# The last attention block weighs behind its three transposes instead of ahead of them

## The chip, the core and the metric

The kernel runs on one NeuronCore of a Trainium2 chip, as one program. The core has five engines that run side by side and meet only through semaphores: TensorE (PE, matrix products, with its weight loads shown apart as PEld), VectorE (DVE), ScalarE (ACT), GpSimd (POOL) and SyncE (SP, here only a DMA queue). Each engine takes its instructions in the order in which the program issued them. Matrix products land in PSUM, eight banks of 128 partitions by 512 floats; DVE and ACT read them out.

The metric is the device time of one execution in microseconds (us), the median of several. "Faster" means less of it.

## What is computed

A stack of four "macaron" layers L0 to L3 over 8 sequences of 512 tokens with 128 features, all in float32. The change touches the attention of layer L3 alone:

```python
def _L3_attn_ref(x, Wq, bq, Wk, bk, Wv, bv):
    q = x @ Wq.T + bq        # likewise k and v; 16 heads of 8 features
    ...
    scores = jnp.einsum('bhqw,bhkw->bhqk', q, k) / jnp.sqrt(jnp.asarray(W, x.dtype))
    scores = jax.nn.softmax(scores, axis=-1)
    scores = jax.nn.softmax(scores, axis=-1)
    h = jnp.einsum('bhqk,bhkw->bhqw', scores, v)
    ...
x = x + 0.5 * _L3_ffn_ref(_layernorm(x, axis=-1), ...)
x = x + _L3_attn_ref(_layernorm(x, axis=-1), ...)
x = x + 0.5 * _L3_ffn_ref(_layernorm(x, axis=-1), ...)
```

The softmax is taken twice, one on top of the other. The feed-forward part picks two of eight experts for each token; its up and down matrices have no activation between them, so the kernel multiplies them together beforehand and applies one 128x128 matrix for each expert.

## The kernel before

`l3_block` (L1414) is the last of four stages. Its attention is cut into 128 units, `units = (b, i, g)`: sequence b of 8, query tile i of 4 (128 queries), head group g of 4 (four heads). One pass of the loop `for n in range(last + 20)` is called unit n here. The order of instructions on PE, ACT, DVE and POOL is exactly the order in which this loop calls its helpers; nothing reorders them. A unit's data takes three passes:

- `score(n, h)`, L1450: four products for the four heads of a group, two for each half h, into a PSUM tile `s` (tag `s1`, two buffers of two banks). Each uses 32 of PE's 128 rows.
- `maximum(n, h)`, L1454, DVE: the row maxima of half h, over 1024 columns.
- `soften(n, h)`, L1461, ACT: the first exponential, two for each half, with row sums. It frees the `s` buffer of its half.
- `norm(n, h)`, L1467 and L1470: reciprocal and scaling on DVE, one of the four scalings on POOL from unit 14 on. Half 1 is done one pass later.
- `turn(n, j)`, L1476, PE: head j's probabilities are transposed, four 128x128 blocks into one PSUM bank `tp` (tag `tp`, three buffers used in turn). Heads 0 to 2 are turned in pass n + 1, head 3 in pass n + 2.
- `again(n)`, L1482, ACT: the second exponential, from `tp` to SBUF tile `p2` (eight buffers), in pass n + 2. It frees the `tp` bank.
- `weigh(n)`, L1492, PE: 16 products of the value weights (32 columns each) with the four `p2` tiles, in pass n + 2, summed into a single PSUM bank `o` that holds the four head groups of one query tile. After the fourth group (g == 3) `o` is copied to the SBUF tile `os` on ACT; `self.scalar` does not issue that copy at once but puts it on the list `self.late`, which `put_off()` issues at two places of the pass.
- `back(b, i)`, L1503 to L1508: in the pass after that copy, `os` is transposed into a `tp` bank, divided by the sums on DVE and added to x on POOL.

Between these the loop calls `works(n)` and `works(n + 0.5)`, which issue the steps of a hand-written timetable: the feed-forward steps of finished sequences (whitening, a transpose `turned`, routing, choosing, and the expert products `yp`, L384, whose readers are L386 on DVE, two or four instructions), and the whitening, transpose, projections and values of the next sequence. Each such step that uses PE takes one buffer from the same ring of three `tp` banks (`bank` with tag `tp`) and gives it back when DVE or ACT has read it. From unit 28 to unit 119 each pass issues an expert step with two readers; every fourth pass also issues `back`.

One pass issues, on PE and in this order: scores of n, turn 3 of n-2, the steps of `works(n)`, the weighing of n-2, the steps of `works(n + 0.5)`, turns 0 to 2 of n-1. On DVE: norm half 1 of n-1, both maxima of n, the readers of the steps, norm half 0 of n. On ACT: the four second exponentials of n-2, the first exponentials of half 0, what was put off, the first exponentials of half 1, what was put off.

The ring of `tp` banks is handed out in the order turn 3, steps, turn 0, turn 1, turn 2. With three banks, each request waits for the reader of the request three before it.

Of the kernel before, what the change touches and what calls it, by code (L numbers as in the profile page):

```python
# [8 lines left out]
F32 = mybir.dt.float32  # L9
I32 = mybir.dt.int32  # L10
AF = mybir.ActivationFunctionType
# [5 lines left out]
P = 128  # L17
# [127 lines left out]
class Net:  # L145
# [1268 lines left out]
    def l3_block(self, w2, w3, out):  # L1414
# [10 lines left out]
        nc, tc, l3 = self.nc, self.tc, self.l3  # L1425
        with ExitStack() as c:
            pool = c.enter_context(tc.tile_pool(name="an", bufs=1))
            wk = c.enter_context(tc.tile_pool(name="anw", bufs=2))
# [13 lines left out]
            scores, maxima, rcs, probs, turns, expos, outs, ats = {}, {}, {}, {}, {}, {}, {}, {}  # L1442

            def score(n, h):
                b, i, g = units[n]
                q, k = qs[b % 2], ks[b % 2]
                s = scores[n, h] = ps.tile([P, 2, 512], F32, tag="s1", name="s1", bufs=2)
                for jj in range(2):
                    cut = slice(32 * (2 * h + jj), 32 * (2 * h + jj) + 32)
                    nc.tensor.matmul(s[:, jj, :], lhsT=q[cut, g, i * P : (i + 1) * P], rhs=k[cut, g, :], start=True, stop=True)  # L1450

            def maximum(n, h):
                nm = maxima[n, h] = wk.tile([P, 2], F32, tag="nm", name="nm", bufs=4)
                nc.vector.tensor_reduce(nm, scores[n, h], AX.X, ALU.max, negate=True)  # L1454

            def soften(n, h):
                s, nm = scores.pop((n, h)), maxima.pop((n, h))
                sm = rcs[n, h] = wk.tile([P, 2], F32, tag="sm", name="sm", bufs=4)
                for jj in range(2):
                    e = wk.tile([P, 512], F32, tag="e", name="e", bufs=12)  # L1460
                    nc.scalar.activation(e, s[:, jj, :], AF.Exp, bias=nm[:, jj : jj + 1], accum_out=sm[:, jj : jj + 1])  # L1461
                    probs.setdefault(n, []).append(e)

            def norm(n, h):

                rc = wk.tile([P, 2], F32, tag="rs", name="rs", bufs=4)
                nc.vector.reciprocal(rc, rcs.pop((n, h)))  # L1467
                for jj in range(2):
                    e = probs[n][2 * h + jj]
                    (nc.gpsimd if h and jj and n >= 14 else nc.vector).tensor_scalar(e, e, rc[:, jj : jj + 1], None, ALU.mult)  # L1470

            def turn(n, j):

                tp = ps.tile([P, 512], F32, name="tp", **turned).rearrange("p (a b) -> p a b", b=P)
                for kt in range(4):
                    nc.tensor.transpose(tp[:, kt, :], probs[n][j][:, kt * P : (kt + 1) * P], self.ident)  # L1476
                turns.setdefault(n, []).append(tp)

            def again(n):

                p = wk.tile([P, 4, P], F32, tag="p2", name="p2", bufs=8)
                nc.scalar.activation(p, turns[n].pop(0), AF.Exp)  # L1482
                expos.setdefault(n, []).append(p)

            def weigh(n):
                b, i, g = units[n]
                if g == 0:
                    outs[b, i] = ps.tile([P, 512], F32, tag="o", name="o")
                o, p2 = outs[b, i], expos.pop(n)
                for kt in range(4):  # L1490
                    for j in range(4):
                        nc.tensor.matmul(  # L1492
                            o[32 * j : 32 * j + 32, g * P : (g + 1) * P], lhsT=vas[b % 2][:, kt, 4 * g + j, :], rhs=p2[j][:, kt, :],
                            start=(kt == 0), stop=(kt == 3))
                if g == 3:
                    outs[b, i] = wk.tile([P, 512], F32, tag="os", name="os")
                    self.scalar(outs[b, i], o, AF.Copy)

            def back(b, i):
                os = outs.pop((b, i))  # L1500
# [9 lines left out]
            units = [(b, i, g) for b in range(NB) for i in range(4) for g in range(4)]  # L1510
            last = len(units)
# [25 lines left out]
            for b in range(NB):  # L1537
                n = 16 * b
                if b:
                    m = max(n - 20, 1)  # L1540
                    self.plan(todo, (m, m + 1, m + 2, m + 3, m + 4, n - 9, n - 7.5, n - 5, n - 4.5), *whiten(b), lambda xn: self.turned(xn, bank, self.longer()),
                              lambda xt, b=b: l3.project(b, 0, xt, bank), lambda xt, b=b: l3.project(b, 1, xt, bank),
                              lambda xt, b=b: l3.values(b, xt, bank))
# [9 lines left out]
            def works(at):  # L1553
                for work in todo.pop(at, ()):
                    work()
# [4 lines left out]
            def put_off():  # L1560
                works, self.late = self.late, []
                for work in works:
                    work()

            self.late = []
            with tc.manual_schedule(engines={*FIXED, mybir.EngineType.Pool}):
                for work in clear:
                    work()
                for n in range(last + 20):
                    here, prev, two = 0 <= n < last, 0 <= n - 1 < last, 0 <= n - 2 < last  # L1570
                    if n == last:
                        spare[0] = dict(tag="s1", bufs=2)
                    if here:
                        score(n, 0)
                        score(n, 1)
                    if two:
                        for j in range(4):
                            again(n - 2)
                            if j == 0:
                                turn(n - 2, 3)  # L1580
                    if prev:
                        norm(n - 1, 1)
                    if here:
                        maximum(n, 0)
                        maximum(n, 1)
                    works(n)
                    if here:
                        soften(n, 0)
                    put_off()
                    if two:  # L1590
                        weigh(n - 2)
                    works(n + 0.5)
                    if prev:
                        for j in range(3):
                            turn(n - 1, j)
                    if here:
                        soften(n, 1)
                        norm(n, 0)
                    put_off()
                assert not todo  # L1600
# [442 lines left out]
```

## Time and profile before

| | us |
|---|---|
| median of 3 runs | 2611.81 (2608.92 to 2611.95) |
| the profiled execution, its own time | 2632.98 |
| its span, first to last instruction | 2631.2 |
| L3 attention units: start of the scores of unit 0, 28, 119, 127 | 1878.35, 2040.45, 2541.76, 2588.95 |
| busy between 2041 and 2484 us (443 us): PE, PEld, DVE, ACT, POOL | 436.7, 291.8, 400.6, 403.6, 223.7 |
| granted TensorE clock in that stretch | 1.00 |

The profile is of one execution. "PE" rows are matrix products, whose ends are modelled and overlap; "PEld" rows are the weight loads ahead of them, whose starts show best when PE went on to the next group. A row of the timeline gives start, length, engine, line, operation, output <- inputs, a count when several were merged, and in brackets the idle time before it with what ended it.

### The profile page before, as it was taken

To read this page: it belongs to the slowest core of one execution; us is meant where nothing else is said; L and a number is where in the kernel's file an instruction comes from. 1 tells how busy PE (TensorE), PEld (TensorE's weight loads), DVE (VectorE), ACT (ScalarE), POOL (GpSimd) and SP (SyncE) were. 2 spreads that over 40 slices of the span, in tenths; PEclk is the share of its full clock that TensorE was granted. 3 is DMA by queue.
4 is the path that set the end of the run, shared out by engine and by line. 5 is a ranking of instruction groups with operands and counts; after the bars stand their busy time and mean duration, and the time that the engine had idled before them with its cause. 6 is when DMAs were issued, how large, how long until landed. Compare 5 with 4: busy or idle time off the path is not lost.

```text
span 2631.2 us, 51301 instructions
## 1 busy us (share of the span) xinstructions
PE 2389.5 (91%) x18184; PEld 1427.7 (54%) x18184; DVE 2024.7 (77%) x5597; ACT 1756.3 (67%) x4393; POOL 1154.0 (44%) x2003
## 2 busy tenths in 40 slices
PE   6858756999999998999999999999899999999997
PEld 6537533344444444566565655556565666666664
DVE  5347348888888866878788787877688989898897
ACT  2135134466677666766757676676598999999984
POOL 5655643244454452163452635332234545454443
PEclk9878877799999999999999999999899999999999
DMA  8121340001010100000000000000000000000000
GB/s 270 51 81 30 93 124 1 18 18 27 19 26 19 34 2 4 1 1 1 1 1 1 1 1 1 1 1 9 9 18 9 10 22 22 10 14 22 22 2 13
DMA packets 72962, 66.51 MB, mean 25 GB/s; under 512 B 15675, under 2 KB 62787, under 8 KB 70563
## 3 DMA queue, kind: packets, MB, share of 16 engines
q1 hardware_dynamic: 68096, 54.88, 7.7%
q0 software_dynamic: 3584, 7.58, 1.0%
q8 instruction: 145, 2.38, 0.4%
q10 hardware_dynamic: 1026, 0.78, 0.1%
q14 instruction: 111, 0.90, 0.1%
HBM read 36.47 MB, written 26.80 MB: 24 GB/s over the span
## 4 chain that ended last, share of the span: by engine, by line
PE 62%; DVE 20%; ACT 9%; POOL 4%; issue 3%; DMA 1%; another core or an unknown queue 0%; SPq 0%; POOLq 0%; DVEq 0%; ACTq 0%
PE tp L1476 8%; PE s L1450 6%; PE s L1290 5%; PE o L1757 4%; PE o L1492 4%; PE o L1320 4%; PE s L1706 4%; PE yp L384 3%; ACT e L1713 3%; PE s L1310 3%; DVE nm L1291 3%; DVE nm L1454 3%; PE tp L1732 2%; PE pp L1674 2%; PE hp L684 2%
## 5 line engine op out<-in xcount | busy, mean ns | idle before, releaser
L1461 ACT ACTIVATE e<-s,nm 128x512 f32<-128x512 f32 x512 | 345.4, 689 | 26.0 <-DVE nm L1454 21.4
L1291 DVE TENSOR_REDUCE nm<-s 128x2 f32<-128x1024 f32 x256 | 301.4, 1218 | 75.9 <-PE s L1310 61.0
L1454 DVE TENSOR_REDUCE nm<-s 128x2 f32<-128x1024 f32 x256 | 301.0, 1217 | 29.6 <-PE s L1450 27.7
L1482 ACT ACTIVATE p<-tp 128x512 f32<-128x512 f32 x512 | 279.3, 618 | 61.6 <-PE tp L1476 61.6
L1312 ACT ACTIVATE pr<-s 128x512 f32<-128x512 f32 x512 | 271.6, 600 | 73.1 <-PE s L1310 69.3
L1476 PE MATMUL tp<-cst,e 128*128 128x128 f32 x2048 | 294.3, 282 | 15.2 <-DVE rs L1467 7.9
L1476 PEld LDWEIGHTS tp<-cst,e 128*128 128x128 f32 x2048 | 221.5, 142 | 153.0 <-issue 86.8
L1470 POOL TENSOR_SCALAR e<-e,rs 128x512 f32<-128x512 f32 x114 | 200.1, 1755 | 229.8 <-DVE rs L1467 191.3
L1290 PE MATMUL s<-k,q 32*128 32x512 f32 x1024 | 279.2, 657 | 18.0 <-DVE nm L1291 14.6
L1310 PE MATMUL s<-q,k 32*128 32x512 f32 x1024 | 290.4, 627 | 5.4 <-DVE at L1333 4.4
L1713 ACT ACTIVATE e<-e,m 128x512 f32<-128x512 f32 (+3 forms) x512 | 286.1, 570 | 12.6 <-DVE m L1710 12.5
L1710 DVE CUSTOM_DVE_ANT_0 e<-s,bias 128x512 f32<-128x512 f32 (+3 forms) x512 | 220.1, 485 | 92.9 <-PE s L1706 92.4
L219 POOL TENSOR_TENSOR d<-st 128x4 f32<-128x4 f32 (+3 forms) x90 | 19.7, 218 | 554.2 <-DVE st L215 356.9
L1734 ACT COPY pt<-tp 128x512 f32<-128x512 f32 x320 | 174.5, 590 | 90.1 <-PE tp L1732 90.1
L386 DVE SCALAR_TENSOR_TENSOR x<-yp,sel,x 128x128 f32<-128x128 f32 x512 | 177.9, 348 | 39.7 <-PE yp L384 26.6
L1470 DVE TENSOR_SCALAR e<-e,rs 128x512 f32<-128x512 f32 x398 | 195.5, 521 | 9.1
L1743 DVE TENSOR_SCALAR e<-e,rc 128x512 f32<-128x512 f32 (+3 forms) x512 | 190.0, 416 | 9.1
L1732 PE MATMUL tp<-cst,e 128*128 128x128 f32 x1280 | 170.9, 278 | 9.8 <-ACT pt L1734 4.0
L1450 PE MATMUL s<-k,q 32*128 32x512 f32 x1024 | 174.8, 651 | 5.1 <-ACT e L1461 2.6
L1706 PE MATMUL s<-qk 64*128 64x512 f32 (+3 forms) x1024 | 173.6, 457 | 2.0 <-DVE m L1710 1.4
L1492 PE MATMUL o<-p,va 128*32 128x128 f32 x4096 | 165.8, 277 | 2.9 <-ACT p L1482 2.9
L1732 PEld LDWEIGHTS tp<-cst,e 128*128 128x128 f32 x1280 | 139.2, 141 | 48.5 <-issue 13.3
(467 smaller groups left out, 4848.0 us busy)
## 6 DMA issues: line engine op xcount, KB each, us to landing
yd<-z SPq DMA_DIRECT2D x8, 1024.0 KB
r<-yd SPq DMA_DIRECT2D x32, 256.0 KB
sk<-pu SPq DMA_DIRECT2D x16, 256.0 KB
k<-sk SPq DMA_DIRECT2D x60, 64.0 KB
w<-in_l_w SPq DMA_DIRECT2D x14, 256.0 KB
xd<-wqkv SPq DMA_DIRECT2D x12, 256.0 KB
x<-in_x SPq DMA_DIRECT2D x8, 256.0 KB
up<-in_l_up SPq DMA_DIRECT2D x8, 256.0 KB
```

Source lines behind the costliest of these rows:

```text
L1290: nc.tensor.matmul(s[:, jj, :], lhsT=q[cut, g, i * P : (i + 1) * P], rhs=k[cut, g, :], start=True, stop=True)
L1291: nc.vector.tensor_reduce(nms[b, g // 2][:, i, 2 * h : 2 * h + 2, g % 2], s, AX.X, ALU.max, negate=True)
L1310: nc.tensor.matmul(s, lhsT=k[cut, g, kt * P : (kt + 1) * P], rhs=q[cut, g, :], start=True, stop=True)
L1450: nc.tensor.matmul(s[:, jj, :], lhsT=q[cut, g, i * P : (i + 1) * P], rhs=k[cut, g, :], start=True, stop=True)
L1454: nc.vector.tensor_reduce(nm, scores[n, h], AX.X, ALU.max, negate=True)
L1461: nc.scalar.activation(e, s[:, jj, :], AF.Exp, bias=nm[:, jj : jj + 1], accum_out=sm[:, jj : jj + 1])
L1470: (nc.gpsimd if h and jj and n >= 14 else nc.vector).tensor_scalar(e, e, rc[:, jj : jj + 1], None, ALU.mult)
L1476: nc.tensor.transpose(tp[:, kt, :], probs[n][j][:, kt * P : (kt + 1) * P], self.ident)
L1482: nc.scalar.activation(p, turns[n].pop(0), AF.Exp)
L1706: nc.tensor.matmul(s[:, jj, 0:w], lhsT=qs[n][cut, i * P : (i + 1) * P], rhs=ks[n][cut, 0:w], start=True, stop=True)
L1713: outs.append(lambda e=e, jj=jj: nc.scalar.activation(e, e, AF.Exp, bias=mins[n][:, jj, i : i + 1], scale=-1.0, accum_out=sums[n][:, jj, i ...
L1732: nc.tensor.transpose(tp[:, k, :], block(n, jj, i, kt), self.ident)
```

## The change

The 16 products of `weigh(n - 2)` are issued behind `works(n + 0.5)` and turns 0 to 2, as the last thing of the pass on PE, so that the scores of n + 1 follow them. The copy of `o` to `os` is taken out of `weigh` into a function `leave`; it is issued in the next pass, on ACT, behind the first of the four second exponentials, and no longer put off. `back` stays in its pass, which is now the pass of the copy.

```diff
@@ weigh(n)
                             start=(kt == 0), stop=(kt == 3))
+
+            def leave(n):
+                b, i, g = units[n]
                 if g == 3:
-                    outs[b, i] = wk.tile([P, 512], F32, tag="os", name="os")
-                    self.scalar(outs[b, i], o, AF.Copy)
+                    o, outs[b, i] = outs[b, i], wk.tile([P, 512], F32, tag="os", name="os")
+                    nc.scalar.copy(outs[b, i], o)
@@ the loop over n
                             again(n - 2)
                             if j == 0:
                                 turn(n - 2, 3)
+                                if n > 2:
+                                    leave(n - 3)
+                    elif 3 <= n < last + 3:
+                        leave(n - 3)
...
                     put_off()
-                    if two:
-                        weigh(n - 2)
                     works(n + 0.5)
                     if prev:
                         for j in range(3):
                             turn(n - 1, j)
+                    if two:
+                        weigh(n - 2)
                     if here:
                         soften(n, 1)
                         norm(n, 0)
```

## Prediction

> **What bounds the kernel now.** I read the page first, for the shares, then the timeline of single units, weight loads and DVE side by side. The page says that PE is the busy engine and shows the groups of the L3 attention:
>
> ```profile
> PE 2389.5 (91%) x18184; PEld 1427.7 (54%) x18184; DVE 2024.7 (77%) x5597; ACT 1756.3 (67%) x4393; POOL 1154.0 (44%) x2003
> ...
> L1482 ACT ACTIVATE p<-tp 128x512 f32<-128x512 f32 x512 | 279.3, 618 | 61.6 <-PE tp L1476 61.6
> ...
> L1492 PE MATMUL o<-p,va 128*32 128x128 f32 x4096 | 165.8, 277 | 2.9 <-ACT p L1482 2.9
> ```
>
> A busy PE may be a waiting PE, so a single unit decides. Unit 44 (scores from 2129.19, next scores 2134.12), weight loads, then ACT:
>
> ```profile
> 2129.19 0.31 PEld L1450 LDWEIGHTS s<-k,q 32*128 32x128 f32 x8 [0.17 <-issue]
> 2130.26 0.42 PEld L1476 LDWEIGHTS tp<-cst,e 128*128 128x128 f32 x4 [0.76 <-issue]
> 2130.65 0.30 PEld L384 LDWEIGHTS yp<-wall,xt 128*128 128x128 f32 x2
> 2131.28 0.15 PEld L1492 LDWEIGHTS o<-p,va 128*32 128x32 f32 x6 [0.33 <-issue]
> 2131.67 0.79 PEld L1492 LDWEIGHTS o<-p,va 128*32 128x32 f32 x26 [0.23 <-ACT p L1482]
> 2132.66 1.29 PEld L1476 LDWEIGHTS tp<-cst,e 128*128 128x128 f32 x12 [0.20 <-issue]
> 2134.12 0.30 PEld L1450 LDWEIGHTS s<-k,q 32*128 32x128 f32 x4 [0.17 <-issue]
> ```
>
> ```profile
> 2131.02 0.60 ACT L1482 ACTIVATE p<-tp 128x512 f32<-128x512 f32 x1 [1.06 <-PE tp L1476]
> ```
>
> PE goes round from scores to scores with one wait: the weighing stops for the fourth second exponential, which needs turn 3, which follows the scores. This is what the change attacks. Now DVE in the same unit, and unit 16 (scores from 1968.97), whose expert step has four readers in place of two:
>
> ```profile
> 2130.37 2.35 DVE L1454 TENSOR_REDUCE nm<-s 128x2 f32<-128x1024 f32 x2 [0.23 <-PE s L1450]
> 2132.64 0.73 DVE L386 SCALAR_TENSOR_TENSOR x<-yp,sel,x 128x128 f32<-128x128 f32 x2
> ```
>
> ```profile
> 1972.44 1.50 DVE L386 SCALAR_TENSOR_TENSOR x<-yp,sel,x 128x128 f32<-128x128 f32 x4
> ```
>
> ```profile
> 1972.50 0.86 PEld L1476 LDWEIGHTS tp<-cst,e 128*128 128x128 f32 x8 [0.20 <-issue]
> 1974.06 0.42 PEld L1476 LDWEIGHTS tp<-cst,e 128*128 128x128 f32 x4 [0.70 <-PE tp L1476]
> 1974.64 0.31 PEld L1450 LDWEIGHTS s<-k,q 32*128 32x128 f32 x8 [0.17 <-issue]
> ```
>
> In unit 16 turns 0 and 1 run, but turn 2 stands still until 1974.06, 0.12 behind the end of L386 at 1973.94: the ring of three gives it the bank of the expert step, which DVE reads only behind both maxima. The label names PE, but the times fit DVE. In unit 44 that bank is free at 2133.37 and turn 2 begins at 2132.66 + 0.86 = 2133.52. The bank was late there too; the weighing stood in the time before it.
>
> **The change, step by step.** I count from a unit's scores S to the next S'.
>
> *Removed from the middle:* weighing, 32 weight loads in 0.81, and the wait for the fourth exponential (0.23 in unit 44). *Added at the end:* the same 0.81 between turn 2 and S'. Its neighbours change: turns to scores (0.17 in the rows) becomes turns to weighing (0.17 is the gap from other 128x128 loads to the weighing in units without an expert step) and weighing to scores. The trace has no weighing followed by scores. Bounds: 0 if the loads slip underneath, 0.20 by the gap from weighing to turns; I take 0.18, near the upper end, since each change of tile shape in these rows shows 0.17 to 0.20. So the tail behind turn 2 grows from 0.17 to 0.17 + 0.80 + 0.18 = 1.15, by 0.98.
>
> The Trainium skill, "TensorEngine Tiling (Array Packing)", Key Properties, says that a change of tiling mode drains the array. The 0.17 to 0.20 agree, and it would put a drain at weighing to scores and take one per unit away in the middle; for a PE that never waited for banks that would be a gain of about 0.2 a unit. By "no drain at the new place" the sum below would be some 20 us less. Against the change speaks "Perfetto Trace Analysis", Identifying Performance Opportunities: a gap that comes back again and again can mean too few PSUM buffers. Unit 16's 0.70 is such a gap, and the change gives the ring no bank, so by this rule the gap stays and the work that filled it is gone.
>
> *What the head start of turns 0 to 2 is worth:* nothing, when turn 2 waits. With one expert step of two readers: maxima from S + 1.18 (2130.37), L386 ends at S + 4.18 (2133.37), turn 2 at S + 4.30, its loads 0.42, then 1.15: S' = S + 5.87. Behind the waiting turn 2 on PE now stand the weighing and the next scores; for those wait maxima, turn 3, and through them every exponential. The next L386 stands behind those maxima, so this is a closed loop, and lateness is not made good in the next unit.
>
> - 48 units (28 to 118) issue just that step. They took 247.9 us, 5.16 each: 18 of them 4.92 as unit 44, the others to 5.4, being early at the scores and waiting for the first exponentials. After: 48 x 5.87 = 281.8, **+33.9**.
> - 18 units add `back`; its second reader ends at S + 4.67 (unit 50), so S' = 4.67 + 0.12 + 0.42 + 1.15 = 6.36. Before 97.4 (5.41 each), after 114.5, **+17.1**.
> - 25 units (five a sequence: transpose, projections, route, values) take two or three banks and already wait for the last. One set took 5.31 + 7.31 + 5.81 + 5.92 + 6.86 = 31.21. By the same rule with their own releases: 6.3 + 7.9 + 6.3 + 6.9 + 7.9 = 35.3. The two that gain part back: the second was 0.5 early at its scores, the third has its routing product sooner. 5 x 4.1, **+20.5**.
> - Units 6 to 27 (128.9 us): 20 of 22 have a step with a bank, at up to +1.0 each; the two without and four whose DVE readers are late for another reason gain part of it back. Estimate from the releases in each unit: **+14**. Units 119 to 126 (47.2 us) the same way: **+6**.
> - Ends: two of units 0 to 5 take a bank, and past unit 127 one weighing moves in front of turn 3 of the last unit: **+2.5**.
>
> *The copy.* 32 copies of 0.61 (L321 before) stay on ACT. They go from behind the first exponentials to behind the first second exponential. I cost the move at nothing: ACT waits there for turn 3 anyway (1.06 in the row above; 0.40 in units that are early). Without that cover it is 32 x 0.6 = 19 us. The weighing of the pass before must be done by then; it ends near S', and the copy is wanted by `back` at S' + 1.5. The single bank `o` is free well before the next weighing. No DMA moves, and POOL and SP queues keep their order; weighing is moved past half-step products and three turns on PE only.
>
> Sum: 33.9 + 17.1 + 20.5 + 14 + 6 + 2.5 = +94. On the profiled execution 2632.98 + 94 = 2727. The runs' median lies 21.2 below that execution, so 2611.8 + 94 = **2706 us** (+3.6%).
>
> **Rivals.**
>
> 1. *Milder loss.* The 48 units stay on their other loop (first exponential, scores, turn 3, fourth second exponential, first exponentials: about 5.3) because DVE reads the bank sooner. For: only 18 of them run at the bank's pace now. Against: DVE order is fixed and maxima follow the scores. Then only the rest pays: 94 - 33.9 = 60, 2672 us.
> 2. *No change.* Weighing was cover for nothing and is cover for nothing: PE has slack before the scores. For: the scores wait for ACT in the units of 5.3. Against: unit 16's 0.70. 2612 us.
> 3. *Faster.* The wait for the fourth exponential was the bound: place, first loads of L1492; price, 0.23 in a unit like 44 plus one change of tile shape less, 0.20: 0.43 x 126 = 54, so 2558 us. It decides if turn 2's bank is free by about S + 3.3, where turn 2 would then want it. For: the 61.6 us that ACT waits for turns. Against: the release at S + 4.18.
> 4. *Worse.* Every unit pays 0.98: 126 x 0.98 = 123, 2735 us.
>
> **How the numbers follow.** Forecast 0.82, milder 0.06, no change 0.04, faster 0.05, worse 0.03. The forecast's own spread: 73 without the gap at weighing to scores (about 115 units x 0.18 = 21 less), 113 if the copy loses its cover (+19). To hold 8 in 10 the range reaches down to the milder case: 2670 to 2725. What a measurement can tell from none is 0.2%, 5 us. Slower 0.91 (forecast, milder, worse), same 0.04, faster 0.05.
>
> **What would show it.** In the profile after, units 28 to 118 at 5.8 to 5.9 without and 6.3 to 6.4 with `back`; weight loads of turn 2 split off and begun 0.1 behind the end of L386; weighing in one group of 32 loads without a wait for ACT; scores no longer waiting for first exponentials; ACT and DVE idle longer, all for PE. The forecast is wrong if turn 2 runs with 0 and 1 in one group, or if the units stay near 5.2.

## The result, and the profile after

| | before, us | after, us |
|---|---|---|
| median | 2610.36 (2606.77 to 2611.95, 4 runs) | 2706.89 (2702.75 to 2711.83, 4 runs) |
| ratio | | 1.0374, 95% interval 1.0361 to 1.0386: slower |
| span of the profiled execution | 2631.2 | 2701.0 |
| scores of unit 0, of unit 127, by their first weight load | 1878.32, 2588.95 | 1850.70, 2657.61 |
| between them | 710.63 | 806.91 |
| from unit 127 to the end of the span | 42.3 | 43.4 |

The attention stage is longer by 96.3 us and the end by 1.1. The spans differ by less, 69.8, since the part ahead of the stage took 27.6 us less in the execution that was profiled after. The medians differ by 96.5. (The 1878.35 for unit 0 in the earlier table is its first product, not its first weight load.)

On the page of the changed kernel, the shares, the shares of the chain that ended last (engines, then lines), and groups; behind them the chain and two of the groups on the page before:

```profile
PE 2334.5 (86%) x18184; PEld 1398.5 (52%) x18184; DVE 2022.7 (75%) x5597; ACT 1766.2 (65%) x4393; POOL 1152.7 (43%) x2003
...
PE 55%; DVE 28%; ACT 9%; POOL 4%; issue 3%; DMA 1%; SPq 0%; ACTq 0%; DVEq 0%; POOLq 0%
DVE nm L1454 10%; PE s L1290 5%; PE s L1450 5%; PE o L1492 5%; PE tp L1476 4%; PE o L1764 4%; PE o L1320 4%; PE s L1713 3%; PE s L1310 3%; ACT e L1720 3%; DVE x L386 3%; DVE nm L1291 3%; PE tp L1739 2%; PE yp L384 2%; PE pp L1681 2%
...
L1476 PE MATMUL tp<-cst,e 128*128 128x128 f32 x2048 | 310.9, 283 | 156.1 <-DVE rs L1467 75.9
L1454 DVE TENSOR_REDUCE nm<-s 128x2 f32<-128x1024 f32 x256 | 301.4, 1219 | 134.0 <-PE s L1450 134.0
...
L1482 ACT ACTIVATE p<-tp 128x512 f32<-128x512 f32 x512 | 283.8, 612 | 133.1 <-PE tp L1476 130.0
```

```profile
PE 62%; DVE 20%; ACT 9%; POOL 4%; issue 3%; DMA 1%; another core or an unknown queue 0%; SPq 0%; POOLq 0%; DVEq 0%; ACTq 0%
...
L1454 DVE TENSOR_REDUCE nm<-s 128x2 f32<-128x1024 f32 x256 | 301.0, 1217 | 29.6 <-PE s L1450 27.7
...
L1476 PE MATMUL tp<-cst,e 128*128 128x128 f32 x2048 | 294.3, 282 | 15.2 <-DVE rs L1467 7.9
```

No engine got more work: the instruction counts are the same, no busy sum grew by more than 10 us, and PE's fell by 55. What grew is waiting. Turns waited 15.2 us before and 156.1 now; the maxima 29.6 and 134.0; the second exponentials 61.6 and 133.1. DVE's share of the chain rose from 20% to 28%, with the maxima (L1454) on top at 10%. The clock is not the cause: from unit 28 to unit 118, where 73.7 of the 96.3 us arise, it was 1.00 in both profiles. Engines wait for each other longer than before, and one unit shows for what.

Unit 44 after, weight loads, from its scores to the next:

```profile
2130.00 0.31 PEld L1450 LDWEIGHTS s<-k,q 32*128 32x128 f32 x8 [0.20 <-issue]
2131.07 0.42 PEld L1476 LDWEIGHTS tp<-cst,e 128*128 128x128 f32 x4 [0.76 <-issue]
2131.46 0.30 PEld L384 LDWEIGHTS yp<-wall,xt 128*128 128x128 f32 x2
2131.79 1.11 PEld L1476 LDWEIGHTS tp<-cst,e 128*128 128x128 f32 x8
2134.29 0.42 PEld L1476 LDWEIGHTS tp<-cst,e 128*128 128x128 f32 x4 [1.40 <-issue]
2134.88 0.81 PEld L1492 LDWEIGHTS o<-p,va 128*32 128x32 f32 x32 [0.17 <-issue]
2135.89 0.31 PEld L1450 LDWEIGHTS s<-k,q 32*128 32x128 f32 x8 [0.20 <-ACT p L1482]
```

The products of turn 2, DVE and ACT in the same unit:

```profile
2134.32 0.63 PE L1476 MATMUL tp<-cst,e 128*128 128x128 f32 x4 [1.19 <-DVE x L386]
```

```profile
2131.18 2.36 DVE L1454 TENSOR_REDUCE nm<-s 128x2 f32<-128x1024 f32 x2 [1.24 <-PE s L1450]
2133.45 0.73 DVE L386 SCALAR_TENSOR_TENSOR x<-yp,sel,x 128x128 f32<-128x128 f32 x2
```

```profile
2131.83 0.60 ACT L1482 ACTIVATE p<-tp 128x512 f32<-128x512 f32 x1 [2.07 <-PE tp L1476]
```

Turns 0 and 1 run early, as the change means them to, and then PE stands for 1.40. The label on the loads is "issue", but L386 ends at 2133.45 + 0.73 = 2134.18 and turn 2 begins 0.11 later; the row of its products names L386 on DVE. The weighing follows in one piece of 0.81, with no wait for ACT, and only behind it the next scores: 5.89 where the same unit took 4.93. The maxima had waited 1.24 for scores, the fourth second exponential 2.07 for turn 3. In every unit from 28 to 118 the weight loads of the scores run in one go (0.31, where before they took up to 0.81); the scores no longer wait for the first exponentials.

### The profile page after: what moved, and what is told of

Its sections match the earlier page's. It is cut to its first block, busy times and chain, and to the rows that moved or that the text cites. A ratio compares the mean times of both kernels' runs of the same rounds, so it can differ in the third digit from the quotient of the medians.

```text
span 2701.0 us, 51296 instructions
## 1 busy us (share of the span) xinstructions
PE 2334.5 (86%) x18184; PEld 1398.5 (52%) x18184; DVE 2022.7 (75%) x5597; ACT 1766.2 (65%) x4393; POOL 1152.7 (43%) x2003
## 4 chain that ended last, share of the span: by engine, by line
PE 55%; DVE 28%; ACT 9%; POOL 4%; issue 3%; DMA 1%; SPq 0%; ACTq 0%; DVEq 0%; POOLq 0%
DVE nm L1454 10%; PE s L1290 5%; PE s L1450 5%; PE o L1492 5%; PE tp L1476 4%; PE o L1764 4%; PE o L1320 4%; PE s L1713 3%; PE s L1310 3%; ACT e L1720 3%; DVE x L386 3%; DVE nm L1291 3%; PE tp L1739 2%; PE yp L384 2%; PE pp L1681 2%
## 5 line engine op out<-in xcount | busy, mean ns | idle before, releaser
L1476 PE MATMUL tp<-cst,e 128*128 128x128 f32 x2048 | 310.9, 283 | 156.1 <-DVE rs L1467 75.9
L1454 DVE TENSOR_REDUCE nm<-s 128x2 f32<-128x1024 f32 x256 | 301.4, 1219 | 134.0 <-PE s L1450 134.0
L1482 ACT ACTIVATE p<-tp 128x512 f32<-128x512 f32 x512 | 283.8, 612 | 133.1 <-PE tp L1476 130.0
L1290 PE MATMUL s<-k,q 32*128 32x512 f32 x1024 | 279.5, 659 | 18.0 <-DVE nm L1291 14.6
L386 DVE SCALAR_TENSOR_TENSOR x<-yp,sel,x 128x128 f32<-128x128 f32 x512 | 177.8, 348 | 39.0 <-PE yp L384 26.0
L1739 PE MATMUL tp<-cst,e 128*128 128x128 f32 x1280 | 170.9, 278 | 9.8 <-ACT pt L1741 4.0
L1739 PEld LDWEIGHTS tp<-cst,e 128*128 128x128 f32 x1280 | 139.2, 141 | 48.5 <-issue 13.1
L1290 PEld LDWEIGHTS s<-k,q 32*128 32x128 f32 x1024 | 88.6, 192 | 137.5 <-DVE nm L1291 100.1
L1450 PE MATMUL s<-k,q 32*128 32x512 f32 x1024 | 154.6, 653 | 5.3 <-ACT e L1461 2.6
```

Of the source, the lines that this page charges most:

```text
L1739: nc.tensor.transpose(tp[:, k, :], block(n, jj, i, kt), self.ident)
```

## The experiments

All times are medians, and ratios are to runs of the kernel before on the same chip: 2609.96 for the four kernels with one part alone or at another place, 2611.07 for the four with something left out, 2643.70 for the three run last. The unit times come from the weight loads of the scores in each profile.

### One part alone

`copy_alone`: the weighing back at its old place, only the copy moved.

```diff
                     put_off()
+                    if two:
+                        weigh(n - 2)
                     works(n + 0.5)
                     if prev:
                         for j in range(3):
                             turn(n - 1, j)
-                    if two:
-                        weigh(n - 2)
```

> Weighing stays at its old place, ahead of the half-step works and the three turns; only the copy of the weighed sums moves into the next pass, behind the first second exponential. Theory (the bare weighing behind turn 2 is the whole loss, the copy stands where ACT waits for turn 3): 2605 to 2617 us, as before. Rival (the copy's new place delays the second exponentials): 32 x 0.6 = 19 us more, 2630.

Measured 2609.17, ratio 0.9997 (0.9987 to 1.0006). The copy's move costs nothing by itself.

`weigh_alone`: the weighing behind the three turns, the copy put off as before.

> Only the weighing moves, behind the three turns; the copy is put off within the same pass as before, so ACT must wait for the weighing's end (about 0.2 us behind the next scores' start) before the second exponentials of the next pass: some 0.45 us later there, 32 times. Theory (the loop goes through maxima, readers, turn 2, weighing, scores and ACT has 0.7 us to spare in it): 2700 to 2715 us, as the changed kernel. Rival (the copy in its new place hides part of the loss, or causes it): 14 us more, 2721, or well under 2700.

Measured 2718.05, ratio 1.0417 (1.0397 to 1.0436). The weighing alone brings the whole loss, and 11 us more than the changed kernel; the theory's bound of 2715 was missed. Unit by unit, the profiles of the two agree to 0.02 from unit 3 to unit 120, and differ by 2.2 in units 121 and 122. So the two were run again side by side, on another chip.

> The changed kernel once more, in one call with the next. 2703 to 2711 us. In the profiles the units 0 to 127 took 806.9 us here and 809.3 with only the weighing moved, all of the 2.4 in units 121 and 122; the medians of the two lay 11 us apart, from different calls. Theory (the copy's place is worth those 2.4): 2 to 5 us between the two. Rival (it is worth 11): 8 to 14 us.

> Only the weighing moves, once more. Theory: 2 to 5 us over the changed kernel of the same call. Rival: 8 to 14 us over it.

Measured 2741.12 and 2743.69 where the kernel before took 2643.70: ratios 1.0370 (1.0356 to 1.0384) and 1.0385 (1.0371 to 1.0399). The gap is 2.6 us, though the two intervals overlap; the 11 did not come back, and the four runs of `weigh_alone` behind it had spread over 14 us (2707.47 to 2721.86). Units 119 to 126 took 54.4 and 56.6, as in the first pair of profiles. Units 28 to 118 took 575.1 and 578.3 in this pair; those 3.1 us lie in four units in which the clock fell (last section), and are not the copy's. The weight loads of turn 2 in unit 121, changed kernel and then `weigh_alone`:

```profile
2621.71 0.47 PEld L1476 LDWEIGHTS tp<-cst,e 128*128 128x128 f32 x4 [1.11 <-ACT p L1482]
```

```profile
2625.56 0.71 PEld L1476 LDWEIGHTS tp<-cst,e 128*128 128x128 f32 x4 [2.64 <-issue]
```

From the scores of the unit (2615.89 and 2618.21) that is 5.82 and 7.35. In the changed kernel turn 2 waits for the first second exponential of the next pass; in the other it waits for the four readers of an expert step, which end at 2625.44. In the changed kernel the same four readers end only at 2623.12, behind the start of turn 2. The semaphores that turn 2 waits for say the same: ACT's alone in the one, those of DVE and PE in the other. So the pool of PSUM tiles handed turn 2 a different bank, by these waits turn 0's instead of the expert step's. The ring is thus not strict, though "The kernel before" and the prediction take it to be so. The two kernels differ only in where the copy stands, and of the units from 3 on only 121 and 122 show a difference.

### The same work at two other places

`between_0_1` and `between_1_2`: the changed kernel with the weighing between two of the turns (k is 1 or 2).

```diff
                     if prev:
-                        for j in range(3):
+                        for j in range(k):
                             turn(n - 1, j)
                     if two:
                         weigh(n - 2)
+                    if prev:
+                        for j in range(k, 3):
+                            turn(n - 1, j)
```

> The changed kernel, but the weighing stands between turn 0 and turn 1. Theory (the loss is that nothing fills the wait of turns 1 and 2 for the bank of an expert step): the weighing fills it again, units of 4.9 to 5.4 us, 2600 to 2615 us in all. Rival (a later weighing costs by itself, by what waits for it, or by its neighbours on PE): 0.4 us or more a unit, over 2650.

> The changed kernel, but the weighing stands between turn 1 and turn 2. Theory: in the 48 units with one expert step only turn 2 waits for its bank, and the weighing fills that wait, 5.2 us each as before; in the 43 units with two or three banks turn 1 waits too, to about 4.3 us behind the scores, and the weighing behind it is bare, about 1.0 us each. Sum 2611 + 43 + some 5 in the first 28 units: 2645 to 2670 us. Rival (a later weighing costs by itself): all units pay, 2700; rival (any place ahead of turn 2 is as good): 2611.

Measured 2607.57, ratio 0.9986 (0.9977 to 0.9995), and 2652.67, ratio 1.0156 (1.0139 to 1.0174). Weight loads of `between_0_1`, unit 44:

```profile
2106.62 0.31 PEld L1450 LDWEIGHTS s<-k,q 32*128 32x128 f32 x8 [0.17 <-issue]
...
2108.40 0.57 PEld L1476 LDWEIGHTS tp<-cst,e 128*128 128x128 f32 x4
2109.15 0.81 PEld L1492 LDWEIGHTS o<-p,va 128*32 128x32 f32 x32 [0.17 <-issue]
2110.16 0.42 PEld L1476 LDWEIGHTS tp<-cst,e 128*128 128x128 f32 x4 [0.20 <-issue]
2110.91 0.42 PEld L1476 LDWEIGHTS tp<-cst,e 128*128 128x128 f32 x4 [0.34 <-PE tp L1476]
2111.50 0.30 PEld L1450 LDWEIGHTS s<-k,q 32*128 32x128 f32 x4 [0.17 <-issue]
```

The weighing stands in the time in which turn 2 waits for its bank; of that wait 0.34 is left and the unit takes 4.88. It also waits for no exponential, since turn 0 runs meanwhile. In `between_1_2` a unit with `back` (unit 50, scores from 2153.73) shows the other case:

```profile
2153.73 0.30 PEld L1450 LDWEIGHTS s<-k,q 32*128 32x128 f32 x4 [0.17 <-ACT e L1461]
...
2156.68 0.42 PEld L1476 LDWEIGHTS tp<-cst,e 128*128 128x128 f32 x4
2158.02 0.42 PEld L1476 LDWEIGHTS tp<-cst,e 128*128 128x128 f32 x4 [0.92 <-PE tp L1476]
2158.61 0.81 PEld L1492 LDWEIGHTS o<-p,va 128*32 128x32 f32 x32 [0.17 <-issue]
2159.62 0.42 PEld L1476 LDWEIGHTS tp<-cst,e 128*128 128x128 f32 x4 [0.20 <-issue]
2160.20 0.31 PEld L1450 LDWEIGHTS s<-k,q 32*128 32x128 f32 x8 [0.17 <-issue]
```

Two banks are taken here, so turn 1 waits already (0.92, to 0.11 behind the end of L386 at 2157.91) and the weighing behind it is bare: the unit takes 6.48, where the kernel before took 5.37. The 48 units with one expert step took 5.08 each (5.17 before), the 18 with `back` 6.56 (5.41), the 25 others 7.06 (6.24; 4.7 us of their sum are falls of the clock, last section). It is not lateness that costs: the weighing costs where it stands behind a turn that waits for DVE, and nothing where it stands ahead of one.

Of the versions that leave nothing out, `between_0_1` and the next are the only ones whose interval lies below the kernel before, `between_0_1` by 0.14%.

`mixed`: `between_0_1`, but in each fourth pass (`n % 4 == 2`) the weighing is ahead of turn 0.

> The weighing stands between turn 0 and turn 1, but ahead of turn 0 in each fourth pass, the one with the transposes of the weighed sums, where two banks are taken and the profile of the version between turn 0 and turn 1 shows 0.2 us more a unit than before (18 units, 3.8 us). Theory (those 18 units lose by it): 3 us less than that version, 2601 to 2606 us. Rival (those units only start earlier against the exponentials, which bound them): no gain, 2606 to 2610 us.

Measured 2638.28 on a chip on which the kernel before took 2643.70: ratio 0.9980 (0.9968 to 0.9992). The intervals of the two versions overlap, so the medians do not tell them apart. In the profiles units 0 to 127 took 705.0 against 705.9, which is not the 3 that the theory named: the 18 units with `back` took 5.56 each, against 5.62 in `between_0_1` and 5.41 before, and their neighbours stayed as they were. Of the 3.8 us that these units had lost 1.1 came back. Neither theory nor rival foresaw that, and what holds the rest is not shown.

### Less of the suspected costs

`half_before`, `half_after`: the same edit in both kernels; only two of the four key blocks are weighed.

```diff
-                for kt in range(4):
+                for kt in range(2):
...
-                            start=(kt == 0), stop=(kt == 3))
+                            start=(kt == 0), stop=(kt == 1))
```

> The kernel before with half of each weighing left out (8 of 16 products, two of the four key blocks), 0.40 us of PE less in each of 128 units. Theory (in the middle of the pass the weighing is cover for the wait of turn 2 for its bank, and the loop over the exponentials is as long): gains of 0.0 to 0.1 us a unit, 2598 to 2611 us. Rival (PE's work bounds the kernel before): 128 x 0.4 = 51 us, 2560.

> The changed kernel with the same half of each weighing left out. Theory (behind turn 2 nothing covers the weighing): 0.40 us less in nearly each unit, 45 to 51 us, 2656 to 2662. Rival (the loss is the changes of shape around the weighing, or the copy): under 10 us less, about 2700.

Measured 2601.85, ratio 0.9967 (0.9957 to 0.9977), and 2657.25, ratio 1.0174 (1.0146 to 1.0201). The same 0.43 us of PE work a unit (loads of 0.38 against 0.81 in unit 44 after) is worth 9 us before and, by the ratios, (1.0374 - 1.0174) x 2611 = 52 us after; in the profiles units 0 to 127 lost 7.2 and 48.5. Before, the 48 units with one expert step gained a quarter of it (5.06 against 5.17); after, all of it (5.46 against 5.89). The weighing was mostly covered and is bare.

`one_reader_before`, `one_reader_after`: the second of two DVE readers is left out.

```diff
-            for e in range(m):
+            for e in range(1 if m == 2 else m):
                 nc.vector.scalar_tensor_tensor(x[:, i, :], yp[:, e, :], ...)
```

> The kernel before with the second of the two DVE readers left out in every expert step of two (96 units), so that x gets half of these experts' products; the bank is free 0.36 us sooner. Theory (before, the bank decides only where two or three banks are taken; elsewhere the weighing or the exponentials do): 18 units gain up to 0.3, 20 units up to 0.36, the rest nothing: 2596 to 2609 us. Rival (bank bound everywhere already): 90 x 0.36 = 32 us, 2579.

> The changed kernel with the same reader left out. Theory (scores, maxima, readers, turn 2, weighing, scores is the loop): 0.36 us less in the 48 and the 18 units and in most of the 25, some 32 us, 2672 to 2679 us; a unit with one expert step takes 5.53. Rival (the place of the weighing costs by itself, whenever the bank is free): no change, 2707.

Measured 2600.82, ratio 0.9963 (0.9949 to 0.9978), and 2671.92, ratio 1.0220 (1.0196 to 1.0244). After, 40 us by the ratios (37.0 in units 0 to 127 of the profiles) where 32 were expected. Unit 44 of `one_reader_after`, DVE and turn 2:

```profile
2134.53 0.34 DVE L386 SCALAR_TENSOR_TENSOR x<-yp,sel,x 128x128 f32<-128x128 f32 x1
```

```profile
2134.93 0.42 PEld L1476 LDWEIGHTS tp<-cst,e 128*128 128x128 f32 x4 [0.95 <-DVE x L386]
```

The 48 units took 5.45, where 5.53 was expected and the changed kernel took 5.89: the reading fell from 0.73 to 0.34, by 0.39, and turn 2 followed it by 0.06, not 0.11. So freeing the bank sooner shortens the changed kernel unit by unit, though neither the weighing nor anything around it was touched; the rival falls. Before, the same edit gave 10 us, nearly all in the units with two or more banks (the 48 took 5.15 against 5.17).

## Why the prediction was right, and where its terms were off

Forecast 2706, measured 2706.9. That the two agree within 1 us is partly luck: the terms are 3.4 us short in sum, and the four runs spread over 9 us. The terms, by the starts of the scores in the two profiles:

| term | predicted | measured |
|---|---|---|
| 48 units, one expert step | 5.87 each, +33.9 | 5.89 each, +35.0 |
| 18 units, and `back` | 6.36 each, +17.1 | 6.38 each, +17.4 |
| 25 units, the set of five | 6.3, 7.9, 6.3, 6.9, 7.9: +20.5 | 6.3, 8.0, 6.3, 6.9, 7.9: +21.2 |
| units 6 to 27 | +14 | +15.3 |
| units 119 to 126 | +6 | +7.2 |
| both ends | +2.5 | +0.2 and +1.1 |
| sum | 94 | 97.4 |

*The bound.* The loop of scores, maxima, readers, turn 2, weighing, scores is shown from both sides: less weighing and a shorter reader each shorten the changed kernel (by 52 and 40 us), the same two edits take only 9 and 10 us off the kernel before, and the weighing put ahead of the waiting turn takes the loss away.

*The head start of the turns* was worth nothing, as costed: with one expert step, two of the three turns started early and the third waited for DVE.

*The gap between weighing and scores*, bounded by 0 and 0.20 and taken as 0.18, is 0.20 in the rows after. With it and the whole 0.81 of the weighing, for which the prediction's sum has 0.80, the tail behind turn 2 is 1.18 and not 1.15; that is the step that made the units 0.02 longer than forecast. So there is a gap at the new change of tile shape too. The rows agree with the Trainium skill, "TensorEngine Tiling (Array Packing)", Key Properties, that such a change drains the array. The change removes one such gap in the middle without profit. That each change of tile shape in its rows shows 0.17 to 0.20 was read too widely: from the scores to turn 3 the loads of unit 44 show 0.76, and from the expert step to the weighing 0.33.

*The repeated gap.* The Trainium skill remarks in "Perfetto Trace Analysis", Optimization Strategy, that a gap that keeps coming back can mean too little SBUF or PSUM for the next tile. This trace agrees: the 1.40 in unit 44 is a wait for the bank. No run here gives the ring a fourth bank, so that one more would close the gap is not shown.

*The copy* at no cost: right alone (0.9997). Together with the moved weighing its place is worth 2.2 us in the profiles, in units 121 and 122, by a choice of the pool that the reasoning with a strict ring could not show.

*The rivals.* The prediction has all but 18 of the 48 units before at "to 5.4"; two took 5.60, which changes no sum. The milder loss fell: all 48 units moved to the bank's pace. The gain fell for the reason given, the release at S + 4.18 (2134.18 - 2130.00 after). "Worse" fell, since units that had been early at the scores paid only the part beyond that: 0.57 in units that had taken 5.32.

*Units without a step* behaved in a way that was not worked out: scores of unit 5 begin 4.07 behind those of unit 4, and their second half waits 0.96 for ACT. Units 4 and 9 took 1.0 and 0.9 less than before, and units 6 and 10 then 1.9 and 1.5 more; of these pairs +0.9 and +0.6 are left, so they cancel only in part. The ends cost about half of what was estimated.

## What to carry to other kernels

In an engine with one fixed order, ask of each piece of work what it stands in front of. Ahead of an instruction that will wait anyway, for a PSUM bank here, it costs little; behind that instruction it is on the path whole, however idle the engine looks. The test is cheap: shorten the piece and see whether the time follows; half the weighing was worth 9 us in the one place and 52 in the other.

## What the runs showed of the hardware that was not expected

- In unit 121 of the changed kernel PE's products waited 0.86 and 0.88 in front of two turns, with 0.63 of products between, and the granted clock was 0.50 in the 1.9 us behind (2622.5 to 2624.4): the 32 weight loads of the weighing took 1.48 against 0.81. The single wait in front of turn 2 in the other units (1.19 by the products, 1.40 by the loads) did not lower it: from 2130 to 2500, some sixty units, it was 1.00.
- Two such waits do not decide it alone. The second unit of each set of five waits 0.72 and 0.87 in the changed kernel, in `weigh_alone_again` and in `between_1_2` alike. The clock fell there in none of the five, in two (units 72 and 104) and in three (40, 72 and 104). Each of these falls lasted 3.41 us and made the unit and the next 1.57 us longer together; two falls in one execution lay a whole number of 3.41 us apart (204.8 us, 60 of them, between units 72 and 104 of `weigh_alone_again`). Whether the place of the waits in that grid decides is not shown. In the kernel before, `copy_alone`, `between_0_1` and `mixed`, where PE waits less, it did not fall between units 3 and 126.
- In two profiles of the same changed kernel, on two chips, the part ahead of this stage took 1850.7 and 1888.6 us, while units 28 to 118 took 575.0 and 575.1. Unit times told versions apart more sharply than spans, but not always: `weigh_alone` took 575.1 and 578.3 there, because of two falls of the clock.
